# Two more GpSimd drains among the last output scatters of a sparse attention kernel

## The chip, the cores and the metric

The kernel runs on one core of a Trainium2 chip. Its metric is the device time of one execution in microseconds, as the median over the runs. A profile of one execution stands beside it; its engines are PE (TensorE matmul), PEld (TensorE weight load), DVE (VectorE), ACT (ScalarE), POOL (GpSimd) and SP (SyncE). A small q behind a name (POOLq) marks an instruction of that engine's sequencer, which the profile doesn't count as busy time.

## The reference

`x` is 2708 x 1024 in float32, `adj` a 2708 x 2708 matrix of zeros and ones with about four ones in a row. One layer of attention runs over a normalised copy of the rows, masked by `adj`, and is added to `x`:

```python
h = jnp.maximum(_layernorm(x, axis=-1), 0.0)
q = h @ W_q.T + b_q
k = h @ W_k.T + b_k
v = h @ W_v.T + b_v
z = (q @ k.T) / math.sqrt(1024)
spare_z = z * adj
spare_z = jnp.where(spare_z == 0.0, -10000.0, spare_z)
x = x + jax.nn.relu(jax.nn.softmax(spare_z, axis=1) @ v)
```

## The kernel before, in words

The rows are cut into 21 tiles of 128 and a rest of 20. The kernel finds the few neighbours of each row, sorts the rows by their number of neighbours, and from there on works on sorted tiles. The weights of q and k are folded into one matrix. For each sorted tile, POOL gathers the neighbours' rows of `h` by indirect DMA (L610), DVE forms the scores and the weighted sum u of the rows, and PE multiplies u by `W_v`. The result goes through relu, gets the rows of `x` added, and is scattered to its places in `out`.

The matmuls are done for pairs of tiles ("units"), seven products of half-size blocks to a pair. There are ten pairs that form q and then ten pairs that form the output; their order is written out by hand in the list `order`, so the last pair but one is tiles 14 and 1, the last pair is tiles 16 and 9, and tile 8 is left alone at the end. `multiply` runs one pair, and calls `after(i)` for i from 0 to 6 between its products; what else has to be issued at a place hangs on the pair's number n and on i.

Three kinds of indirect DMA belong to the output, all of them issued by POOL, in one queue. `add_x` (L1109) gathers rows of `x` and adds them onto a finished tile y in SBUF. `gather` (L612) fetches rows of `x` for the last pair and for tile 8, where DVE does the addition itself (`joined_x`, L1144). `scatter` (L808) writes a tile's rows to `out`; each is noted in the list `outs`. For all pairs but the last, `add_due` issues the two steps one after the other at a place of the next pair, and the scatter of a tile comes behind the `add_x` of the tile after it. The last pair has its own results, in `ends`: tile 16 (`ya`) is scattered in `c12`, tile 9 (`yb`) in `c21`. Tile 8 (`y_alone`) is scattered in two halves of 512 columns (`scatter_half`, L1366).

Behind the last half a flag is read by every engine (L1388), which decides whether a general, slow version has to run; with this input it is skipped (L1389). At the program's end (L1562), SP waits for the landing of all DMAs and for the engines' last work, each engine issues a drain, and all of them meet at a barrier. The drains at the program's start and end are put there by the framework; the kernel itself issues none.

`tc.issue_after(a)` makes what is issued inside it stand behind the instruction `a` in the order of the program; `outs[-1]` is the scatter that was issued last.

Of the kernel before, what the change touches and what calls it, by code (L numbers as in the profile page):

```python
# [65 lines left out]
def tile_preln_masked_attention(  # L66
# [12 lines left out]
    nc = tc.nc  # L79
# [527 lines left out]
    def gather(dst, src, t, w, n, skip=False):  # L607
        off = bass.IndirectOffsetOnAxis(ap=ptab.bitcast(U32)[:n, t, w:w + 1], axis=0)
        if skip:
            return nc.gpsimd.indirect_dma_start(out=dst, out_offset=None, in_=src, in_offset=off,  # L610
                                                bounds_check=N - 1, oob_is_err=False)
        return nc.gpsimd.indirect_dma_start(out=dst, out_offset=None, in_=src, in_offset=off)  # L612
# [142 lines left out]
    def banks_for(row):  # L755

        return_ = []
        for h in range(NH):
            return_.append(psum.tile([P, NB], FT, tag="acc", name=f"ps{h}"))
            nc.scalar.copy(return_[h], row[:, h * NB:(h + 1) * NB])  # L760
        return return_
# [43 lines left out]
    outs = []  # L805

    def scatter(y, t, n):
        to = nc.gpsimd.indirect_dma_start(  # L808
            out=out, out_offset=bass.IndirectOffsetOnAxis(ap=ptab.bitcast(U32)[:n, t, SLOTS:SLOTS + 1], axis=0),
            in_=y[:n], in_offset=None)  # L810
        for other in outs:
            tc.declare_no_dep(to.ins, other.ins, reason="rows of a permutation")
        outs.append(to)
# [230 lines left out]
    def multiply(n, results, after):  # L1044


        X, Z = banks_of.pop(n)
        ops = ops_of.pop(n)[0]
        Y, p5 = opened_of.pop(n)
        after(0)  # L1050
        after(1)
        products.append(add_block(Y, ops["s2"], T[:, 1]))
        u2 = small("u2")
        nc.scalar.copy(u2, Y)
        after(2)
        add_block(X, ops["a12"], M[:, 1, 0])
        results[0](X)
        after(3)
        products.append(add_block(Z, ops["s4"], M[:, 1, 1]))
        results[2](Z, u2)  # L1060
        after(4)
        products.append(add_block(Y, ops["s3"], T[:, 2]))
        results[1](Y, p5)
        after(5)
        between(n)
        add_block(Y, ops["a22"], T[:, 3])
        results[3](Y)
        after(6)
# [42 lines left out]
    def o_results(ta, tb):  # L1111
        ya = work.tile([P, D], FT, tag="q", name=f"y_{ta}", bufs=4)
        yb = work.tile([P, D], FT, tag="q", name=f"y_{tb}", bufs=4)
        if (ta, tb) == o_pairs[-1]:
            return ends(ya, ta, yb, tb)

        def c11(X):
            nc.scalar.activation(ya[:, lo], X, AF.Relu)

        def c22(Y, p5):  # L1120
            nc.vector.tensor_add(p5, copied(Y), p5)
            nc.scalar.activation(yb[:, hi], p5, AF.Relu)

        def c12(Z, u2):
            nc.vector.tensor_add(u2, Z, u2)
            nc.scalar.activation(ya[:, hi], u2, AF.Relu)  # L1126
            if ta == NT - 2:

                nc.sync.dma_start(tail_dram, ya[P - 1:, :])
            due.append((now[0], 5, ya, ta))  # L1130

        def c21(Y):
            nc.scalar.activation(yb[:, lo], Y, AF.Relu)
            due.append((now[0] + 1, 1, yb, tb))

        return c11, c22, c12, c21

    def ends(ya, ta, yb, tb):

        send(gather(ya, x, ta, SLOTS, P))  # L1140
        gather(yb, x, tb, SLOTS, P)

        def joined_x(y, cols, a):
            nc.vector.scalar_tensor_tensor(y[:, cols], a, 0.0, y[:, cols], op0=ALU.max, op1=ALU.add)  # L1144

        def c11(X):
            joined_x(ya, lo, X)

        def c22(Y, p5):
            nc.vector.tensor_add(p5, Y, p5)  # L1150
            joined_x(yb, hi, p5)

        def c12(Z, u2):
            nc.vector.tensor_add(u2, Z, u2)
            joined_x(ya, hi, u2)
            scatter(ya, ta, P)

        def c21(Y):
            joined_x(yb, lo, Y)
            scatter(yb, tb, P)  # L1160

        return c11, c22, c12, c21
# [10 lines left out]
    def send(behind, stay=0):  # L1173

        while len(sent) > stay:
            with tc.issue_after(behind.ins):
                scatter(*sent.pop(0))
# [16 lines left out]
    units = [("q",) + p for p in q_pairs] + [("o",) + p for p in o_pairs]  # L1194
# [34 lines left out]
    for n, unit in enumerate(units):  # L1229
# [13 lines left out]
        def after(i):  # L1243
# [81 lines left out]
                single["rows"], = load_rows(("o", alone))  # L1325
            if nxt is None and i == 3:
                single["banks"] = banks_for(bp_sb)
            if n == last_q - 1 and i == 4:

                nc.sync.dma_start(bp_sb, bv.to_broadcast([P, D]))  # L1330
# [235 lines left out]
```

## Time and profile before

| | |
|---|---|
| median of 3 runs | 637.19 us (636.75 to 637.22) |
| span of the profiled execution, first to last instruction | 635.2 us |
| the profiled execution's own time | not given beside its span; the median lies 2.0 us above it |
| PE busy | 624.2 us (98%) |
| POOL busy | 367.3 us (58%) |
| mean granted TensorE clock | 0.996 |
| indirect and other DMAs of POOL's queue (q0) | 86.02 MB |

Busy time is the union of an engine's instructions. Instructions of a sequencer (waits for semaphores, branches, drains) are not in it, so an engine can be held by them and be shown as idle; they are listed when the profile is asked for the line that issues them, with their number, the shortest, median and longest duration in ns, and the first and last start.

### The profile page before, as it was taken

The page shows a single profiled execution, that of the slowest core. Times are in us where ns is not written, and L with a number is a line of the kernel's source. Part 1 is how long each engine was busy: PE and PEld are TensorE (multiplying, and loading weights), DVE is VectorE, ACT ScalarE, POOL GpSimd, SP SyncE. Part 2 cuts the span into 40 slices and gives each one's busy share as a digit, 9 for nine tenths or more (in the row PEclk, how much of TensorE's full clock was granted, in tenths as well). Part 3 has the DMA queues.
Part 4 walks back from the last instruction along what each step waited for, and adds up shares of the span by engine and source line. Part 5 has one row for each costly group of instructions (what it writes and reads, how often), then busy time and mean ns, then how long its engine had stood idle before and what let it go on. Part 6 is the DMA issues. An engine that isn't in the chain of part 4 may idle for free.

```text
span 635.2 us, 6138 instructions
## 1 busy us (share of the span) xinstructions
PE 624.2 (98%) x1627; PEld 316.4 (50%) x1627; DVE 523.9 (82%) x1020; ACT 285.9 (45%) x423; POOL 367.3 (58%) x397
## 2 busy tenths in 40 slices
PE   9999999999999999999999999999999999999993
PEld 5777766444444544444444444444444444444441
DVE  5999888998896755997889999999899999898231
ACT  3538985749667553424341244343343342432200
POOL 2639960885877277564742644586678868622421
PEclk9999999999999999999999999999999999999998
DMA  8999997598796539996599997999999989993851
GB/s 340 407 369 310 342 356 288 203 325 310 261 360 237 182 118 323 342 351 220 188 295 365 307 399 227 322 346 294 386 354 289 336 276 284 278 269 80 242 189 37
DMA packets 62497, 181.16 MB, mean 285 GB/s; under 512 B 10055, under 2 KB 17047, under 8 KB 61688
## 3 DMA queue, kind: packets, MB, share of 16 engines
q0 software_dynamic: 27088, 86.02, 42.6%
q1 hardware_dynamic: 29434, 73.63, 33.2%
q10 hardware_dynamic: 5934, 21.06, 8.5%
q8 instruction: 15, 0.25, 0.1%
q14 instruction: 26, 0.21, 0.1%
HBM read 148.27 MB, written 42.31 MB: 300 GB/s over the span
## 4 chain that ended last, share of the span: by engine, by line
PE 98%; POOL 0%; DVE 0%; POOLq 0%; issue 0%
PE ps L1010 45%; PE psy L1010 32%; PE ps_y L476 6%; PE ps_z L476 4%; PE ps_x L476 4%; PE pt L415 4%; PE ps_y L511 1%; PE ps_h L1222 0%; PE ps_v L594 0%; DVE y_alone L1382 0%; POOL out_dram L1366 0%; POOLq L1388 0%; POOL hsum L121 0%; PE ps_all L680 0%; PE ps_in L678 0%
## 5 line engine op out<-in xcount | busy, mean ns | idle before, releaser
L610 POOL DMA_INDIRECT g<-h_dram,tab x94 | 119.6, 1272 | 62.1 <-ACT u L912 19.1
L1010 PE MATMUL ps<-M,a 128*128 128x512 f32 x320 | 144.0, 593 | 0.0
L1010 PE MATMUL psy<-wlow,s 128*128 128x512 f32 x320 | 143.9, 593 | 0.0
L863 DVE SCALAR_TENSOR_TENSOR junk<-g,pq 128x1024 uint8<-128x1024 f32 x93 | 113.7, 1223 | 12.8 <-DMA g<-h_dram,tab 8.9
L1010 PE MATMUL ps<-M,s 128*128 128x512 f32 x240 | 107.9, 593 | 0.0
L1010 PEld LDWEIGHTS ps<-M,a 128*128 128x128 f32 x320 | 59.9, 190 | 70.7 <-issue 70.0
L1010 PEld LDWEIGHTS psy<-wlow,s 128*128 128x128 f32 x320 | 59.8, 190 | 70.0 <-issue 69.1
L923 DVE SCALAR_TENSOR_TENSOR u<-g,coef,u 128x1024 f32<-128x1024 f32 x69 | 88.4, 1282 | 6.9 <-ACT u L912 5.8
L389 DVE FIND_INDEX8 at<-ones,adj 128x8 uint32<-128x685 f32 (+1 forms) x88 | 74.5, 864 | 0.0
L1010 PEld LDWEIGHTS ps<-M,s 128*128 128x128 f32 x240 | 45.6, 190 | 57.1 <-issue 55.9
L1010 PE MATMUL psy<-wlow,a 128*128 128x512 f32 x160 | 71.9, 593 | 0.0
L368 ACT ACTIVATE sized<-adj 128x2708 uint8<-128x2708 f32 (+1 forms) x22 | 54.3, 2467 | 7.3 <-DMA adj<-in_adj_dram 6.0
L298 POOL TENSOR_TENSOR hsum<-hsum,x 128x256 f32<-128x256 f32 (+1 forms) x56 | 38.6, 726 | 26.2 <-DVE wlow L444 21.6
L1109 POOL DMA_INDIRECT y<-in_x_dram,tab x19 | 32.7, 1723 | 30.5 <-ACT y L1126 15.7
L1010 PEld LDWEIGHTS psy<-wlow,a 128*128 128x128 f32 x160 | 30.5, 190 | 38.2 <-issue 37.5
L1010 PE MATMUL ps<-wlow,s 128*128 128x512 f32 x80 | 36.0, 592 | 0.0
L912 ACT ACTIVATE u<-g,coef 128x1024 f32<-128x1024 f32 x18 | 20.7, 1148 | 29.9 <-DVE coef L911 29.8
L808 POOL DMA_INDIRECT out_dram<-y,tab x21 | 25.3, 1206 | 15.2 <-DVE flag L1357 7.1
L626 POOL DMA_INDIRECT tab_dram<-tab,pos_i x22 | 21.9, 993 | 18.8 <-DVE pos_i L689 13.3
L276 ACT ACTIVATE x<-x,r 128x1024 f32<-128x1024 f32 (+1 forms) x22 | 25.9, 1233 | 7.2 <-POOL r L266 7.2
L944 ACT COPY v<-u 128x1024 f32<-128x1024 f32 x13 | 13.6, 1046 | 32.5 <-DVE u L923 28.2
L476 PE MATMUL ps_y<-wlow 128*128 128x512 f32 x64 | 27.6, 593 | 0.0
(252 smaller groups left out, 851.7 us busy)
## 6 DMA issues: line engine op xcount, KB each, us to landing
adj<-in_adj_dram SPq DMA_DIRECT2D x21, 1354.0 KB, 10.4
x<-in_x_dram SPq DMA_DIRECT2D x21, 512.0 KB, 11.0
h_dram<-x ACTq DMA_DIRECT2D x21, 512.0 KB, 7.3
u_dram<-v ACTq DMA_DIRECT2D x13, 512.0 KB, 6.6
or<-u_dram SPq DMA_DIRECT2D x52, 128.0 KB, 6.4
q_late<-q SPq DMA_DIRECT2D x12, 512.0 KB, 7.1
pq<-q_late POOLq DMA_DIRECT2D x12, 512.0 KB, 8.0
M<-in_wv_dram SPq DMA_DIRECT2D x4, 1024.0 KB, 10.4
```

The costliest lines, as they stand in the source:

```text
L276: nc.scalar.activation(xs[i][:n], xs[i][:n], AF.Relu, bias=r[:n, 4, i:i + 1], scale=r[:n, 3, i:i + 1])
L298: small.append(nc.gpsimd.tensor_add(hsum[:n, cols], hsum[:n, cols], xt[:n, cols]))
L368: nc.scalar.activation(sized[:n], a[:n, :, :PW], AF.Abs, accum_out=total[:n, t:t + 1])
L389: nc.vector.max_index(at[:n, k - first_k, g, :], ones[:n, 0:8], a[:n, g, :])
L415: nc.tensor.transpose(pt[:, c, :], xt[:, k * P:(k + 1) * P], ident)
L476: mm = nc.tensor.matmul(bank, a_tile(o + H * a[0], a[1], i), b(o), start=first and o == 0, stop=(o == H - 1), skip_group_check=True)
L610: return nc.gpsimd.indirect_dma_start(out=dst, out_offset=None, in_=src, in_offset=off, bounds_check=N - 1, oob_is_err=False)
L808: to = nc.gpsimd.indirect_dma_start(out=out, out_offset=bass.IndirectOffsetOnAxis(ap=ptab.bitcast(U32)[:n, t, SLOTS:SLOTS + 1], axis=0), i ...
L863: chained(lambda: nc.vector.scalar_tensor_tensor(junk, g_of[t][s], 1.0, tq[t], op0=ALU.mult, op1=ALU.mult, accum_out=zall[:, t, s:s + 1]))
L923: chained(lambda: nc.vector.scalar_tensor_tensor(u, g_of[t][s], coef[:, s:s + 1], u, op0=ALU.mult, op1=ALU.add))
L1010: mm = nc.tensor.matmul(bank, a[:, c, :], b[:, c, :], start=False, stop=(c == 3), skip_group_check=True)
L1109: return nc.gpsimd.indirect_dma_start(out=y[:n], out_offset=None, in_=x, in_offset=off, compute_op=ALU.add)
```

## The change

Two drains of GpSimd are added. The first stands in `after`, in the last pair but one (n = 18, i = 2), behind the scatter that was issued last there, that of tile 11. The second stands in `ends`, behind the scatter of tile 16. No other line is changed.

```diff
@@ in c12 of ends
             nc.vector.tensor_add(u2, Z, u2)
             joined_x(ya, hi, u2)
             scatter(ya, ta, P)
+            with tc.issue_after(outs[-1].ins):
+                nc.gpsimd.drain()
@@ in after
             if nxt is None and i == 3:
                 single["banks"] = banks_for(bp_sb)
+            if (n, i) == (len(units) - 2, 2):
+                with tc.issue_after(outs[-1].ins):
+                    nc.gpsimd.drain()
             if n == last_q - 1 and i == 4:
```

A listing of POOL's instructions leaves out those that only wait, drains among them, so the two show in it by the buffers' running numbers alone, which count every instruction. In the built program the first drain stands between the scatter of tile 11 and the `add_x` of tile 14 (y_14_3607), and carries no semaphore. This is POOL's queue from that `add_x` on, the rows of before marked - and the rows of the changed program +:

```order
 L1109 DMA y_14_3607<-in_x_dram,tab_97 128x1024 [waits DMASW5_49,DMASW0_49,Activation_49]
 L808 DMA out_0_dram<-y_15_3447,tab_97 2708x1024 [waits DMASW4_49,DMASW1_49]
-L612 DMA y_16_3705<-in_x_dram,tab_97 128x1024 [waits DMASW2_49,DMASW1_49]
+L612 DMA y_16_3706<-in_x_dram,tab_97 128x1024 [waits DMASW2_49,DMASW1_49]
 L808 DMA out_0_dram<-y_10_3448,tab_97 2708x1024 [waits DMASW6_49,DMASW3_49]
 L808 DMA out_0_dram<-y_14_3607,tab_97 2708x1024 [waits DMASW0_49]
 L1109 DMA y_1_3608<-in_x_dram,tab_97 128x1024 [waits DMASW7_49,Activation_49]
-L612 DMA y_9_3706<-in_x_dram,tab_97 128x1024 [waits DMASW3_49]
-L612 DMA y_alone_3775<-in_x_dram,tab_97 128x1024 [waits DMASW4_49]
+L612 DMA y_9_3707<-in_x_dram,tab_97 128x1024 [waits DMASW3_49]
+L612 DMA y_alone_3777<-in_x_dram,tab_97 128x1024 [waits DMASW4_49]
```

Buffers made before the first drain keep their numbers, those made behind it are one higher, and those behind the second two higher. The order and the waits are the same. The second drain stands between the scatters of tile 16 (y_16) and tile 9 (y_9), again without a semaphore:

```order
L808 DMA out_0_dram<-y_1_3608,tab_97 2708x1024 [waits DMASW5_49]
L808 DMA out_0_dram<-y_16_3705,tab_97 2708x1024 [waits DMASW2_49,DVE_49]
L808 DMA out_0_dram<-y_9_3706,tab_97 2708x1024 [waits DMASW6_49,DVE_49]
L1366 DMA out_0_dram<-y_alone_3775,half_i_3772 5416x512 [waits DMASW7_49,DVE_49]
L1366 DMA out_0_dram<-y_alone_3775,half_i_3772 5416x512 [waits DVE_49]
```

These are the rows of before; in the changed program the same place reads:

```order
L808 DMA out_0_dram<-y_1_3608,tab_97 2708x1024 [waits DMASW5_49]
L808 DMA out_0_dram<-y_16_3706,tab_97 2708x1024 [waits DMASW2_49,DVE_49]
L808 DMA out_0_dram<-y_9_3707,tab_97 2708x1024 [waits DMASW6_49,DVE_49]
L1371 DMA out_0_dram<-y_alone_3777,half_i_3774 5416x512 [waits DMASW7_49,DVE_49]
L1371 DMA out_0_dram<-y_alone_3777,half_i_3774 5416x512 [waits DVE_49]
```

Three DMAs stand behind the second drain: the scatter of tile 9 and the two halves of tile 8. No instruction of another engine is added, removed or moved, and no wait has changed. DMASW0 to DMASW7 are the eight semaphores that POOL's DMAs use in turn to tell of their landing.

## The prediction

> **What bounds the kernel now.** I read the page first, for what fills the span.
>
> ```profile
> span 635.2 us, 6138 instructions
> PE 624.2 (98%) x1627; PEld 316.4 (50%) x1627; DVE 523.9 (82%) x1020; ACT 285.9 (45%) x423; POOL 367.3 (58%) x397
> q0 software_dynamic: 27088, 86.02, 42.6%
> ```
>
> PE is busy for 624.2 of 635.2 us, so up to the last matmul nothing that POOL does can be worth anything unless PE waits for it. What is left is the end. The chain of work that ended last, from 614 us on (start, length, what), has these pieces:
>
> ```profile
> 615.00 10.42 PE ps L1010 x24
> 625.45 0.70 DVE y_alone L1382
> 626.68 0.69 POOL out_dram L1366
> ```
>
> The last matmul ends at 625.4, DVE adds the last half of tile 8 up to 626.15, and POOL issues its scatter up to 627.37. There the chain ends, and the span goes on for 7.8 us, in which no engine is shown as busy. Since drains and semaphores are the sequencers', I asked for the framework's last line, L1562, from 627 to 631 us (number, shortest/median/longest in ns, first and last start):
>
> ```profile
> L1562 SPq EVENT_SEMAPHORE  x12: 27/28/28, 629.7 to 630.4; - x12
> L1562 SPq DRAIN  x2: 7/10/13, 630.4 to 630.5; - x2
> L1562 POOLq DRAIN  x1: 7122/7122/7122, 627.2 to 627.2; - x1
> L1562 DVEq DRAIN  x1: 17/17/17, 629.2 to 629.2; - x1
> ```
>
> Then for the same line in the last microsecond, and over the whole span:
>
> ```profile
> L1562 POOLq EVENT_SEMAPHORE  x4: 17/17/17, 634.4 to 635.1; - x4
> L1562 POOLq DRAIN  x3: 46/109/7122, 627.2 to 634.9; - x3
> L1562 ACTq DRAIN  x2: 8/8/8, 616.5 to 634.6; - x2
> L1562 PEldq DRAIN  x2: 8/8/8, 625.6 to 634.7; - x2
> ```
>
> One instruction ends the kernel: POOL's drain, which starts at 627.2 and takes 7.12 us, to 634.36. Every other engine is through earlier: ACT at 616.5, PE at 625.6, DVE at 629.2, and SP, which has waited for the last landing, at 630.5. POOL passes the barrier at 634.4, and the rest takes 0.8 us. From 630.5 to 634.4, 3.9 us, everybody waits for POOL alone.
>
> What does it wait for? The last scatter, by the answers for its line (first row) and for SP's waits (second row):
>
> ```profile
> DMA to landing us min/median/max: 3.2/3.2/3.2
> SPq L1562 <- DMA out_dram<-y_alone,half_i: 10.3, 1, 10.3
> ```
>
> It is issued at 626.41, lands 3.2 us later, at 629.65, and SP goes on at once. So 4.7 us of POOL's drain lie behind the landing of everything. The last windows confirm that nothing moves then (length, busy time and number for PE, PEld, DVE, ACT and POOL, clock, DMA share, GB/s):
>
> ```profile
> 627.38:630.50 3.12, 0.00 (x0) 0.00 (x0) 0.00 (x0) 0.00 (x0) 0.00 (x0) 0.98 0.24 89
> 630.50:634.36 3.86, 0.00 (x0) 0.00 (x0) 0.00 (x0) 0.00 (x0) 0.00 (x0) 0.50 0.00 0
> ```
>
> Whatever POOL does is its own, and no row shows it. Other drains of POOL give the comparison. Two at the end, directly behind the long one, took 109 and 46 ns (median and shortest in the row above). The one at the program's start, behind four small memsets and before any DMA, is this one:
>
> ```profile
> L1555 POOLq DRAIN  x1: 184/184/184, 0.4 to 0.4; - x1
> ```
>
> So a drain of POOL is no fixed cost: 0.05 to 0.18 us with nothing or next to nothing behind it since the last drain, 7.12 us with all of the kernel's 86 MB of software DMAs behind it. What makes the difference lies in the DMAs issued since the drain before.
>
> **The change, part by part.** It adds two instructions and moves none. POOL's timeline has these rows around the two places (start, length, engine, line, operation, idle time before and what ended it):
>
> ```profile
> 573.03 1.00 POOL L808 DMA_INDIRECT out_dram<-y,tab  x1 [0.30 <-issue]
> 586.05 1.70 POOL L1109 DMA_INDIRECT y<-in_x_dram,tab  x1 [12.03 <-ACT y L1126]
> 595.62 0.97 POOL L808 DMA_INDIRECT out_dram<-y,tab  x1 [0.30 <-issue]
> 596.89 0.97 POOL L808 DMA_INDIRECT out_dram<-y,tab  x1 [0.30 <-issue]
> 598.16 1.60 POOL L1109 DMA_INDIRECT y<-in_x_dram,tab  x1 [0.30 <-issue]
> 607.86 0.96 POOL L808 DMA_INDIRECT out_dram<-y,tab  x1 [0.77 <-DVE many L1354]
> 615.89 0.95 POOL L808 DMA_INDIRECT out_dram<-y,tab  x1 [7.06 <-DVE flag L1357]
> 623.77 0.97 POOL L1366 DMA_INDIRECT out_dram<-y_alone,half_i  x1 [6.93 <-DVE y_alone L1379]
> 626.41 0.96 POOL L1366 DMA_INDIRECT out_dram<-y_alone,half_i  x1 [1.67 <-DVE y_alone L1382]
> ```
>
> The first drain comes behind the scatter at 573.03, so at 574.03, and the next in the queue, the addition of x to tile 14, waits for ACT until 586.05. The cover is 12.0 us. The longest price that the trace has is 7.12 us, to 581.2; if the drain first waits for what is in flight and then takes the 4.7 us seen behind the last landing, the scatter's landing decides:
>
> ```profile
> DMA to landing us min/median/max: 5.7/5.7/5.7
> ```
>
> 573.03 + 5.7 + 4.7 = 583.4. Either way it costs nothing. Behind it in the queue stand that addition, the scatters of tiles 15, 10, 14 and 1, and the gathers for tiles 16, 9 and 8; they start as before.
>
> The second drain comes behind the scatter of tile 16, at 608.82. Next is the scatter of tile 9, at 615.89: a cover of 7.06 us. At the full price the drain ends at 615.9. The landing rule, with the landings of the two scatters issued from 606 to 609 us, gives a little more:
>
> ```profile
> DMA to landing us min/median/max: 4.8/5.1/5.3
> ```
>
> 607.86 + 4.8 + 4.7 = 617.4, so tile 9 is scattered 1.5 us later. Nobody waits for that: the next thing in the queue, the first half of tile 8, comes at 623.77 and waits for DVE. Both ends of this term are zero on the path; the least (0.05 us) and the full price differ only off it.
>
> The term that counts is the last drain. Behind the second drain POOL issues three DMAs, 512 KB and twice 256 KB, 1.05 of q0's 86.02 MB. Its price lies between 0.05 us, the drains with nothing since, and 7.12 us. By the amount of DMA it stands next to the lower end: 7.12 x 1.05 / 86.02 = 0.09 us, an estimate from these two rows. I take it as short, and don't need to know how short: SP is through at 630.5 in any case, since it waits for the landing at 629.65, which doesn't move. Any last drain under 630.5 - 627.4 = 3.1 us is hidden behind SP.
>
> The Trainium skill speaks against this in one place. VectorE: DVE Perf Modes, section "The DRAIN you can't avoid", says that the drains which the runtime puts around a kernel take a constant 12 ns or so on all five engines. By that there would be nothing to save and the sum would be 637.2. The rows agree for SP, ACT, PE and DVE (7 to 17 ns), and not for POOL (7122 ns); the measurement decides.
>
> What a drain waits for, the same notes say in PSUM — Partial Sum Buffer, section on the semaphore on a trailing nop: until the engine is fully idle. The trace agrees in that POOL's is the only long one, but shows POOL itself as idle, so no run here shows yet what it is busy with.
>
> The sum: the barrier forms when SP gets there, at 630.5 instead of 634.4, and what follows takes 0.8 us as before. Span 635.2 - 3.9 = 631.3. The profiled span lies 2.0 us below the median of 637.19; with the same 2.0 the time is **633.3 us**. Less than that is not in it: DVE, PE and the landing stand where they stood, so 3.9 us is the most that can go.
>
> **The rivals.** A difference of 0.2%, 1.3 us, is about what a measurement of this kernel can tell from no change.
>
> First, the drain is a procedure of fixed length as soon as any DMA has been issued since the last one, say because it asks each DMA queue in turn. For it: the 4.7 us behind the last landing, in which nothing moves, look like a routine. Against it, a little: indirect DMAs follow each other at 1.27 us (595.62, 596.89, 598.16), so no single one leaves 7 us of work that has to be done before the next; but a routine that only a drain runs fits that too. Then the last drain stays at 7.1 us, the two new ones stand in their gaps, and the time is 637.2. With this goes the case that a drain isn't where it should be, which the built program all but excludes.
>
> Second, the backlog is real but short: only the last DMAs count, one for each of the eight completion semaphores. Then three of eight are left for the last drain: 3/8 x 4.7 = 1.8 us behind the landing at 629.65, to 631.4, which is 0.9 us later than SP. The time is 633.3 + 0.9 = 634.2, and any price between this and the full one lands between 634 and 637.
>
> Third, slower: a drain in the middle of traffic takes far longer than one at the quiet end, and holds the queue. The place is the second drain, with the scatter of tile 9 and both halves of tile 8 behind it, each start 1.27 us after the other. The last of them starts at 626.41 now, so it decides from 626.41 - 2 x 1.27 = 623.9 on, which is a drain of 15 us from 608.8, twice the longest in the trace. If it takes 14.2 us, twice that price, but from the landing at 612.7 on, it ends at 626.9, the last scatter starts at 629.4, 3.0 us late, and with a last drain that stays long the time is 640.2. For it speaks only that no drain beside traffic is in the trace; against it, that DMA traffic in that stretch is light (0.25 of the DMA engines' time from 608.83 to 615.89):
>
> ```profile
> 608.83:615.89 7.06, 7.06 (x20) 3.24 (x19) 1.45 (x3) 0.58 (x1) 0.00 (x1) 1.00 0.25 102
> ```
>
> **How the numbers follow.** My forecast, 633.3 us with 632.8 to 634.0 around it, has a chance of 0.66: the rows of short drains are three, they all follow a stretch without DMAs, and three DMAs are close to none. The second rival has 0.14, the first 0.11, the third 0.09. Faster by over 0.2% are the forecast and the second rival, 0.80; within 0.2% the first, 0.11; slower the third, 0.09. The range starts half a microsecond under the forecast, about the spread of the runs shown, and reaches to 636.8 through the second rival, so that the other two, 0.20, are left out.
>
> **What would show it.** In the changed profile, a POOLq DRAIN should appear at the two new lines, at about 574 and 609 us, the first one the longest. The one at the last line should be under 3.1 us, SP's at 630.5 should be the last before the barrier, and the span should be about 631.3. A last drain of 7 us again means the first rival; one that ends a little behind SP the second; a scatter of a half of tile 8 that starts later than 623.8 or 626.4 the third. A matmul that ends later than 625.4 would mean that I have missed a wait of PE.

## The result, and the profile after

The changed kernel takes 633.67 us (median of 4 runs, 632.80 to 634.41) where before takes 637.15 us. The ratio is 0.9946, with an interval of 0.9932 to 0.9960: 3.5 us less, where 3.9 was forecast. The profiled execution took 634.37 us, with a span of 632.7.

The page has the same work on every engine:

```profile
span 632.7 us, 6140 instructions
PE 625.3 (99%) x1627; PEld 315.7 (50%) x1627; DVE 523.9 (83%) x1020; ACT 286.0 (45%) x423; POOL 368.9 (58%) x397
```

The chain at the end is the same as before, each piece 1.46 us later (start, length, what):

```profile
616.46 10.42 PE ps L1010 x24
626.90 0.70 DVE y_alone L1387
628.14 0.69 POOL out_dram L1371
```

What comes behind it has changed. The answers for the two new lines and for the framework's last line (now L1567), over the whole span, then for that line from 627 to 632 us:

```profile
L1332 POOLq DRAIN  x1: 11585/11585/11585, 572.6 to 572.6; - x1
L1158 POOLq DRAIN  x1: 5158/5158/5158, 609.4 to 609.4; - x1
L1567 POOLq DRAIN  x3: 46/109/2442, 628.7 to 632.4; - x3
L1567 SPq EVENT_SEMAPHORE  x13: 17/28/28, 631.0 to 632.0; - x13
L1567 SPq DRAIN  x2: 7/10/13, 631.8 to 631.8; - x2
L1567 POOLq EVENT_SEMAPHORE  x2: 17/17/17, 631.9 to 631.9; - x2
```

The last drain takes 2.44 us instead of 7.12 and is over at 631.15. SP, which goes on at 631.0 when the last scatter has landed, is through at 631.8, and POOL passes the barrier right behind it, at 631.9: SP is the last now. From the end of the last matmul to the end of the span it is 632.66 - 626.87 = 5.8 us, where before had 635.22 - 625.41 = 9.8: 4.0 us less.

The 1.46 us by which everything is later in this execution arose long before the first new drain: the trace has the 60th matmul 0.81 us late and the 480th, at 187 us, 1.46 us late, and the distance stays so to the end. The second step is a wait for a load of `adj`, from the chain of 160 to 190 us:

```profile
166.99 10.30 DMA adj<-in_adj_dram
177.32 3.48 DVE at L389 x5
```

In before, the chain of that stretch is matmuls alone. Two of the four runs have spans of 632.7 and 632.6 us, the other two 631.3 and 631.1; the forecast span was 631.3. Only the first of them was profiled, so the profile shows the early delay for that one alone.

POOL's timeline around the new drains:

```profile
574.49 1.00 POOL L808 DMA_INDIRECT out_dram<-y,tab  x1 [0.30 <-issue]
587.48 1.69 POOL L1109 DMA_INDIRECT y<-in_x_dram,tab  x1 [11.99 <-ACT y L1126]
609.61 0.97 POOL L808 DMA_INDIRECT out_dram<-y,tab  x1 [0.77 <-DVE many L1359]
617.35 0.95 POOL L808 DMA_INDIRECT out_dram<-y,tab  x1 [6.77 <-DVE flag L1362]
625.23 0.96 POOL L1371 DMA_INDIRECT out_dram<-y_alone,half_i  x1 [6.93 <-DVE y_alone L1384]
627.87 0.96 POOL L1371 DMA_INDIRECT out_dram<-y_alone,half_i  x1 [1.67 <-DVE y_alone L1387]
```

Take off 1.46 us, and the starts are 573.03, 586.02, 608.15, 615.89, 623.77 and 626.41: those of before to 0.03 us, except the scatter of tile 16, which is 0.29 us later. Some DMAs between the two drains are 0.1 to 0.3 us later too; from the scatter of tile 9 on nothing on POOL has moved, and both drains stand in gaps that were there. A drain's record starts when the sequencer gets to it, which here is before the DMAs ahead of it have run (572.6 against 574.49), so its end says more than its length: 584.2 and 614.5.

### The profile page after: what moved, and what is told of

Same layout as the page of the kernel before. It is cut to its first block, busy times and chain, and to the rows that moved or that the text cites. A ratio compares the mean times of both kernels' runs of the same rounds, so it can differ in the third digit from the quotient of the medians.

```text
span 632.7 us, 6140 instructions
## 1 busy us (share of the span) xinstructions
PE 625.3 (99%) x1627; PEld 315.7 (50%) x1627; DVE 523.9 (83%) x1020; ACT 286.0 (45%) x423; POOL 368.9 (58%) x397
## 4 chain that ended last, share of the span: by engine, by line
PE 94%; DVE 3%; DMA 2%; issue 0%; POOL 0%; POOLq 0%; SPq 0%
PE ps L1010 43%; PE psy L1010 31%; PE ps_y L476 7%; PE ps_x L476 4%; PE ps_z L476 4%; PE pt L415 4%; DMA adj<-in_adj_dram 2%; DVE at L389 1%; PE ps_y L511 1%; DVE st L237 1%; PE ps_h L1224 0%; PE ps_v L594 0%; DVE sort L684 0%; DVE cand L407 0%; DVE y_alone L1387 0%
## 5 line engine op out<-in xcount | busy, mean ns | idle before, releaser
L1010 PEld LDWEIGHTS ps<-M,a 128*128 128x128 f32 x320 | 59.8, 190 | 70.8 <-issue 69.6
L1109 POOL DMA_INDIRECT y<-in_x_dram,tab x19 | 35.2, 1853 | 30.4 <-ACT y L1126 15.7
L760 ACT COPY ps<-bp_sb 128x512 f32<-128x512 f32 x42 | 24.6, 596 | 6.8 <-DVE y L1144 6.3
## 6 DMA issues: line engine op xcount, KB each, us to landing
x<-in_x_dram SPq DMA_DIRECT2D x21, 512.0 KB, 10.7
```

What stands on the lines that cost most here:

```text
L1010: mm = nc.tensor.matmul(bank, a[:, c, :], b[:, c, :], start=False, stop=(c == 3), skip_group_check=True)
L1109: return nc.gpsimd.indirect_dma_start(out=y[:n], out_offset=None, in_=x, in_offset=off, compute_op=ALU.add)
```

## The experiments

All of them are read from one number: how long behind the last landing of POOL's DMAs a drain ends. The landings are in the trace's record of semaphore updates, which is finer than the views. The theory at the start was that of a backlog: a drain waits for what is in flight to land, and then works off something for each of POOL's DMAs since the drain before. The rivals were a warm-up that is paid once, and a price for the last few DMAs alone. Chips differ, so kernels are compared with before on their own chip. The deleted and added lines below are shown against the changed kernel.

**The change again.** No edit.

> The changed kernel once more. Its profiled run had all matmuls end 1.46 us later than before, at 626.88 instead of 625.42 us, long before and after the new drains alike. If that is the luck of a run, the ratio here lies near 0.994 (633.3 us) and the place of the last matmul differs from profile to profile; if the change causes it, the last matmul ends at 626.9 again. The last drain takes about 2.4 us by every theory.

635.43 us against 641.02 of before on that chip, 0.9911 (0.9881 to 0.9941). The last drain ended 0.16 us behind the landing. In its profile, as in those of the other kernels, the last matmul ends elsewhere each time (629.4 us here, 627.3 in the repetition below, 625.3 with the ten small DMAs), so the 1.46 us were a run's, not the change's, as the two shorter spans above say too. Before spread over 7 us on that chip, so the change was run again on another:

> The changed kernel again, with more rounds, since the chip of its first repetition scattered by 7 us in the kernel before too. Backlog theory: ratio 0.993 to 0.995 to before; the last drain ends 0.16 us behind the landing, and SP's drain is the last before the barrier.

635.21 us against 639.49, 0.9939 (0.9916 to 0.9962), with 0.16 us again, and SP last.

**One of the two alone.** The second drain taken out of the change:

```diff
             scatter(ya, ta, P)
-            with tc.issue_after(outs[-1].ins):
-                nc.gpsimd.drain()
```

> The second new drain is left out. Backlog theory (a drain waits for the landing of what is in flight, and then needs some 22 ns for each of POOL's DMAs since the last drain, 4.71 us for 213 before): 13 DMAs are left for the last drain, 0.3 to 0.6 us behind the landing; SP needs 0.84 us behind the landing, so the time is that of the changed kernel. Rival that the second drain is what matters, because the last few DMAs cost most: the last drain ends over 0.84 us behind the landing and the time is up to 1 us over the changed kernel's.

> The first new drain alone, with more rounds. Backlog theory: 13 DMAs are left, 0.04 + 13 x 0.0412 = 0.58 us behind the landing, under SP's 0.84; the time is that of the changed kernel within 0.2%. If the second drain is worth something by itself, this kernel is slower than the changed one.

Ratios of 0.9919 (0.9888 to 0.9950) and 0.9944 (0.9926 to 0.9963): not to be told from the whole change. The last drain ends 0.58 us behind the landing in both, before SP (first profile; SP's drains at 635.8, POOL's at 632.7 + 2.98 = 635.6):

```profile
L1565 POOLq DRAIN  x3: 46/109/2983, 632.7 to 636.5; - x3
L1565 SPq DRAIN  x3: 7/7/13, 635.8 to 636.1; - x3
```

And the first drain taken out:

```diff
-            if (n, i) == (len(units) - 2, 2):
-                with tc.issue_after(outs[-1].ins):
-                    nc.gpsimd.drain()
```

> The first new drain is left out. Backlog theory: the second one has 210 DMAs behind it and needs 4.6 us from the last landing on (612.7 to 614.1 us), so it ends at 617.3 to 618.7 us and tile 9 is scattered up to 1.5 us later; the last drain ends 0.16 us behind the landing as with both, and the time is that of the changed kernel. If a drain so near to the end disturbs what follows, the last scatter starts later than 2.5 us behind the last matmul's start of eviction and the time is over the changed kernel's.

0.9935 (0.9911 to 0.9958), again the same. The second drain now ends 4.59 us behind the landing and the last one 0.17 us:

```profile
L1158 POOLq DRAIN  x1: 9225/9225/9225, 609.5 to 609.5; - x1
L1564 POOLq DRAIN  x3: 46/109/2638, 629.5 to 633.4; - x3
```

It runs to 609.5 + 9.2 = 618.7 us, and tile 9 is scattered at 619.5, 1.3 us later against the last matmul than in before; the next in the queue comes 6.6 us behind that, so it costs nothing. One drain is enough, and within these intervals it doesn't matter which of the two.

**One drain four pairs earlier.**

```diff
-            if (n, i) == (len(units) - 2, 2):
+            if (n, i) == (14, 2):
```

with the second drain left out.

> One drain alone, four pairs earlier (n = 14, i = 2), behind the scatter that is issued last there; 148 of POOL's 213 DMAs stand before it and 65 behind it. Backlog theory: the last drain ends 65 x 22 ns = 1.4 us behind the landing, 0.6 us later than SP, so the time is 0.5 to 0.6 us over the changed kernel's and some 3.3 us under before. Warm-up theory (the first drain behind DMAs pays some 4.2 us once, whatever their number, and later ones are short): the last drain ends 0.2 us behind the landing and the time is the changed kernel's. The new drain itself stands among gathers: by the backlog theory it ends 148 x 22 ns = 3.3 us behind its last landing and holds POOL's queue so long; whether PE feels that is open.

1.0027 (1.0002 to 1.0051): no faster than before and perhaps a little slower, where both theories had at least 3 us less. Two things came together in the profile. The last drain ends 3.01 us behind the landing, not 1.4, and 2.2 us later than SP:

```profile
L1565 POOLq DRAIN  x3: 46/109/5505, 631.6 to 637.7; - x3
L1565 SPq DRAIN  x3: 7/7/13, 634.9 to 637.4; - x3
```

So the warm-up theory falls (it had 0.2 us), and so does the 22 ns: it is 46 ns for each of 65 DMAs here, and 14 ns for each of the 148 before the first drain, which ended 2.05 us behind its landing. And the new drain held POOL's queue: from 476.3, where the scatter is issued, to 485.7, with gathers waiting behind it. (In this kernel the built program also puts the `add_x` that follows ahead of two of these gathers, which it comes behind in before.)

```profile
475.24 1.03 POOL L808 DMA_INDIRECT out_dram<-y,tab  x1 [0.30 <-issue]
485.73 1.73 POOL L1109 DMA_INDIRECT y<-in_x_dram,tab  x1 [9.46 <-issue]
```

PE loses time behind it only near the end, where it waits twice for DVE:

```profile
611.03 3.70 PE L1010 MATMUL ps<-M,T_alone 128*128 128x512 f32 x8 [0.76 <-DVE T_alone L705]
615.58 3.70 PE L1010 MATMUL psy<-wlow,a 128*128 128x512 f32 x8 [0.85 <-DVE p L1150]
```

Of the other kernels' profiles only that with a drain in every pair, below, has these two waits (1.03 and 0.85 us). That they come from the held queue is the likely reading, but the way from the drain to DVE's lateness, over 120 us, was not followed.

**Where the backlog begins.** Two single drains, behind the 77th and the 100th of POOL's 213 DMAs, with the others left out:

```diff
-            if (n, i) == (len(units) - 2, 2):
-                with tc.issue_after(outs[-1].ins):
+            if (n, i) == (7, 4):        # (10, 4) in the second kernel
+                with tc.issue_after(gathered[-1].ins):
                     nc.gpsimd.drain()
```

> One drain alone, behind the 77th of POOL's 213 DMAs (n = 7, i = 4). The runs so far gave, from the last landing to the drain's end, 2.05 us behind 148 DMAs, 4.18 behind 200, 4.59 behind 210 and 4.71 behind 213: 41 ns for each of the last 65, but only 14 ns for each of the first 148. Two readings. Either the early DMAs leave next to nothing and the backlog begins at about the 99th: then this drain ends under 0.2 us behind the landing. Or every DMA leaves 41 ns and POOL clears the backlog by itself once, at about the 99th (148 less 2.05 us / 41 ns): then it ends 77 x 41 ns = 3.2 us behind the landing.

> One drain alone, behind the 100th DMA (n = 10, i = 4). By both readings it ends under 0.3 us behind the landing; 4.1 us would say that neither holds. The last drain then has 113 DMAs since and ends 113 x 41 ns = 4.6 us behind the last landing, as before, so the time is that of before: a drain that comes too early brings nothing.

Behind 77 DMAs the drain ended 3.20 us after the landing, behind 100 it took 4.14 us, which neither reading had. Every DMA counts from the first on, 41 ns each, and nothing had come off the price by the 100th. The last drains had 136 and 113 DMAs since and ended 1.19 and 4.67 us behind the landing:

```profile
L1330 POOLq DRAIN  x1: 9733/9733/9733, 309.2 to 309.2; - x1
L1565 POOLq DRAIN  x3: 46/109/3383, 627.1 to 631.1; - x3
```

```profile
L1330 POOLq DRAIN  x1: 20492/20492/20492, 370.3 to 370.3; - x1
L1565 POOLq DRAIN  x3: 46/109/6834, 629.9 to 637.3; - x3
```

The first rows are of the drain at 77, the other two of that at 100. 113 DMAs cost nearly what 213 cost in before, 136 much less, as if POOL dropped most of its backlog somewhere without a drain. One run each gave 633.04 us with the drain at 77 and 639.32 with that at 100 (before 637.25). The drain at 100 brings nothing at the end and holds POOL for 18 us in the middle. The drain at 77 was run again:

> One drain behind the 77th DMA, in the q pairs, with more rounds. Its single look left a last drain of 1.19 us behind the landing with 136 DMAs since, as if POOL had cleared some 107 of them by itself. If that repeats, SP is overtaken by 0.36 us and the time is 0.3 to 0.4 us over the changed kernel's, that is 0.9935 to 0.9955 of before; if it doesn't, the last drain ends 0.04 + 136 x 0.0412 = 5.6 us behind the landing and the time is over that of before.

0.9948 (0.9926 to 0.9971), and 1.19 us again: SP is overtaken by 0.35 us. In time it can't be told from the change.

**Number or size.** Ten DMAs of 16 bytes behind the second drain:

```diff
+                drained = nc.gpsimd.drain()
+            for i in range(10):
+                with tc.issue_after(drained.ins):
+                    nc.gpsimd.dma_start(tiny_dram[i:i + 1, :], minus[0:1, 0:4])
```

> The changed kernel with 10 more DMAs of 16 bytes each behind the second drain, on a scratch row that nobody reads. If the last drain's price goes by the number of DMAs, it ends 0.16 + 10 x 41 ns = 0.57 us behind the landing instead of 0.16; if it goes by bytes or by data descriptors, at 0.16 to 0.2 us. Both are less than SP's 0.84 us, so the time is the changed kernel's.

The last drain ended 0.58 us behind the landing, as with the 13 DMAs of 256 and 512 KB behind the first drain alone. It is the number that counts, not the bytes. One run gave 632.22 us.

```profile
L1162 POOL DMA_DIRECT2D tiny_dram<-minus x10: 502/509/582, 613.0 to 617.6; - x10
L1571 POOLq DRAIN  x3: 46/109/2747, 626.8 to 630.2; - x3
```

**A drain in every pair.**

```diff
-            if (n, i) == (len(units) - 2, 2):
+            if i == 2 and 12 <= n < len(units) - 1:
```

> The first drain in each of the last seven pairs but one (n = 12 to 18, i = 2) instead of once, and the second as in the change. Backlog theory: each ends 41 ns per DMA since the drain before it behind its last landing, 0.5 to 0.7 us for 12 to 17 DMAs. Each also waits for the landing of what is in flight, 5 to 8 us in which POOL issues nothing; among the gathers of the sums that holds DVE, and if DVE's slack is used up, PE. If POOL's queue has slack there, the time is the changed kernel's; if not, up to 6 x 5 = 30 us over it. The single drain at n = 14 stood in a traffic like this and its kernel had a time 0.3% over before.

1.0179 (1.0145 to 1.0212): 11 us slower. The seven drains on that line take 8.9 to 16.9 us each, of which only 0.25 to 1.04 us lie behind the last landing. The rows of the timeline show POOL idle from 428.3 to 437.5 us around the first of them, and the last two rows a window of 80 us in this kernel and in before:

```profile
L1332 POOLq DRAIN  x7: 8852/13230/16946, 422.4 to 588.9; - x7
426.64 1.67 POOL L808 DMA_INDIRECT out_dram<-y,tab  x1 [0.30 <-issue]
437.54 0.56 POOL L833 DMA_DIRECT2D pq<-q_late  x1 [9.24 <-DVE u L923]
480.00:560.00 80.00, 70.83 (x189) 32.74 (x188) 62.05 (x98) 22.79 (x41) 48.92 (x38) 0.96 0.79 241
480.00:560.00 80.00, 80.00 (x224) 38.14 (x223) 74.57 (x112) 30.53 (x52) 59.02 (x46) 1.00 0.94 294
```

PE is busy for 70.8 us of it, where before has all 80. The gathers come late, DVE's sums with them, and PE waits. So the slack of POOL's queue among these gathers is small. (Here too the built program orders some of POOL's DMAs otherwise than in before.)

**The end of every kernel.** What happens early in a run doesn't touch the stretch from the last matmul to the end of the span, so it shows best what a drain does there. It is 9.8 us in before and 9.5 with the drain at 100, whose last drains end 4.7 us behind the landing. It is 8.2 in the early one, where that is 3.0 us. In all the others, where the last drain ends before SP or 0.35 us behind it, it is 5.2 to 6.2 us.

**The drains side by side.** The number of DMAs since the drain before, and where the drain ends behind the last landing, with the line 0.04 + 0.0412 n beside it. Left out are drains that repeat one of these cases, and the rest of each pair's; they agree with it, or with the line, to 0.02 us:

| drain | DMAs n | measured us | line us |
|---|---|---|---|
| change, last | 3 | 0.16 | 0.16 |
| each pair, n = 18 | 5 | 0.25 | 0.25 |
| change, second | 10 | 0.46 | 0.45 |
| only first, last | 13 | 0.58 | 0.58 |
| ten small DMAs, last | 13 | 0.58 | 0.58 |
| each pair, n = 15 | 17 | 0.74 | 0.74 |
| early one, last | 65 | 3.01 | 2.72 |
| drain at 77 | 77 | 3.20 | 3.21 |
| drain at 100 | 100 | 4.14 | 4.16 |
| drain at 100, last | 113 | 4.67 | 4.70 |
| each pair, first | 123 | 1.04 | 5.11 |
| drain at 77, last | 136 | 1.19 | 5.64 |
| early one | 148 | 2.05 | 6.14 |
| change, first | 200 | 4.18 | 8.28 |
| only second | 210 | 4.59 | 8.69 |
| before, last | 213 | 4.71 | 8.82 |

Up to 113 the line holds to 0.03 us, but for one drain that is 0.3 us over it, which stays unexplained. From 123 on the price is that of 99 to 108 DMAs fewer. That POOL clears so many at once, once more than 113 are open and before 123 are, fits all of them; it isn't shown, and what exactly is worked off for each DMA isn't either. In before the 100th to 123rd DMA take 0.6 to 2.6 us each to issue, so no single issue holds the 4 us that clearing a hundred would take at 41 ns; POOL's idle time there could.

## Why the prediction was right, point by point

**What bounds the end.** Right. POOL's drain was what all waited for; made shorter, it gave SP the last place, at the distance from the landing that the prediction read off (0.84 us), and the stretch behind the last matmul lost 4.0 us where 3.9 was summed.

**The number.** 633.67 us against 633.3, and part of this nearness is luck. The sum adds 2.0 us to the profiled span; in the runs on record a time lies 1.7 to 1.9 us above its span, so the profiled execution of before lay 0.1 to 0.3 us under the median, and the sum carried that along. Against that, the median span came out 0.65 us over the forecast 631.3, since two of the four runs were 1.4 us longer than the others. In the profiled one this arose early, part of it at the load of `adj`. So a matmul did end later than 625.4 us, the sign that the prediction gave for an overlooked wait of PE, but that wait stands long before the drains and differs from run to run.

**The first drain in its gap.** Right, by the landing rule: the scatter landed at 580.0 and the drain ended 4.18 us later, at 584.2, with 3.3 us left to the next DMA. The price of 7.12 us taken as a block was no bound at all, since the wait for landings comes on top of the work.

**The second drain.** Right that it costs nothing; the bound was too high. It ended at 614.5, less than 0.5 us behind its landing, and tile 9's scatter wasn't late.

**The last drain.** The step that was mis-sized, without effect. The prediction set its price by bytes, 0.09 us, and left out that it waits for the landing first. It took 2.44 us, of which 2.28 lie before the landing, and then 0.16 us for three DMAs, by their number and not their size; that 0.09 lies near 0.16 is luck. All of it lies under the 3.1 us that the prediction had shown to be hidden.

**The rivals.** A procedure of fixed length falls: 0.16 to 4.71 us. A price for the last eight alone falls: it had 1.8 us for three DMAs, which cost 0.16, and 77 cost 3.2 us. A drain that holds the queue is real, but not at the place named: the second drain was over 10.7 us before the next half of tile 8, while drains among the gathers cost 11 us in seven pairs.

**The notes.** The Trainium skill gives about 12 ns for each of the runtime's drains, on all five engines (VectorE: DVE Perf Modes, "The DRAIN you can't avoid"). The framework's drains here agree in all these runs for SP, ACT, PE and DVE (7 to 17 ns), and never for POOL's drain behind DMAs.

## What to carry to other kernels

Look behind the last instruction that the chain names: a sequencer's drain isn't busy time, and at the end of a kernel it can be the longest thing there. If GpSimd issues many DMAs, one drain of it in a late gap, long enough for the landing of what is in flight and the backlog, takes the backlog off the end; a drain where its queue is full of gathers can cost all that it brings or more (the early one, the drain in every pair), though the one at 77 cost nothing that the runs could tell. How much there is to gain is read from the distance between the last drain's end and that of the next engine to reach the barrier.

## What the runs showed of the hardware

A GpSimd drain waits until its DMAs have landed, and then takes 0.04 us plus 41 ns for each DMA that GpSimd has issued since the last drain, 16 bytes or 512 KB alike. For 3 to 113 DMAs this holds to 0.03 us in runs on several chips, but for one drain that took 0.3 us more. With 123 to 213 of them since, it costs as if about a hundred had been cleared before.
